# A transformer block on one core: the second MLP starts its halves with products 1 and 2 of both half groups, ends them in another order, keeps pieces of down back, and moves the last layer norm

## The chip, the core and the metric

The kernel runs on one core of a Trainium2 chip. The core has a matrix engine (TensorE, PE in the profile), VectorE (DVE), ScalarE (ACT), GpSimd (POOL) and SyncE (SP), which here only issues DMA transfers. Each engine works through its own queue of instructions in order and waits at semaphores. The metric is the device time of one execution in microseconds. Three runs of the kernel before took 3165.64, 3166.33 and 3169.07 us, so the median is 3166.33 us.

## What is computed

One block over 2048 tokens of width 512, in float32: an MLP, attention with 16 heads of 32, and the same MLP once more, each behind a layer norm and added to its input.

```python
x = x + 0.5 * ffn(layernorm(x))
x = x + attention(layernorm(x))
x = x + 0.5 * ffn(layernorm(x))

def ffn(x):                      # Wg, Wu: 4096 x 512, Wd: 512 x 4096, unpacked from 4-bit codes
    gate, up = x @ Wg.T, x @ Wu.T
    inter = gelu_tanh(gate) * up
    return inter @ Wd.T
```

The first MLP unpacks the weights and keeps them in DRAM; the second MLP, which the change is about, reads them from there.

## The kernel before

**Products.** Every matrix product of the second MLP is done by a scheme that needs 7 products of blocks instead of 8 and pays with additions of blocks. For gate and up it is applied twice: an outer product i in 1..7 is itself made of 7 inner products y in 1..7. The tokens are handled in two halves of 1024. The 4096 columns of the hidden layer are 8 groups g of two half groups h, so a half has 8 x 2 x 7 = 112 outer products. `problems` (L598) lists them, and two at a time form a **pair**: a half has NP = 56 pairs, numbered n = 0..55 in the first half and 56..111 in the second.

**A pair** (`pair`, L705) issues its 7 inner products. Three banks of PSUM, d, f and e, hold the results. Products 1, 6, 7 and 4 go into bank d one after the other, and between them d is read: ScalarE copies it to u1 after product 1 and to u2 after product 6 (L754, L767), VectorE adds d and u5 into the output after product 7 (L770), and only then may product 4 write it, which ScalarE copies out (L776). With pieces of down to interleave the order is 1, 5, 2, 6, pieces "a", 7, 3, pieces "b", 4; without them 1, 5, 6, 2, 7, 3, 4. After the k-th product, the hooks of step k are issued.

**Operands.** The tokens of a half lie transposed in four tiles, called b1, b2, ts and t4 in the code. The outer product i reads x block `(None, 0, 1, 3, 6, 2, 5, 4)[i]` (L699 ff., `factors`): products 1 and 2 read blocks 0 and 1, which are b1 itself; product 3 reads a block of b2; product 5 the difference t1 in b2; 6 and 7 the sums in ts; 4 the one in t4. `outer_sums` (L616) makes ts, t4 and t1 from b1 and b2 with the steps t3, t2, t4, t1. `Tokens.inner(t)` (L684) makes the sums that the inner products 5, 6, 7 and 4 need for the t-th tile; they are called first (b1), second (b2), third (ts) and fourth (t4).

**After a pair.** `recombine(n - 1)` (L777) adds outer products of the pair before into each other (L791), applies gelu on ScalarE (L794) and multiplies gate by up into `inter` blocks (L803). These steps go to steps 1, 4 and 6 of the next pair.

**Down.** When a group is done, `down` (L835) forms four sums of `inter` blocks (L845 to L848, in the tile s, of which there is one) and yields 14 **pieces** of 8 matmuls each (L866). The pieces of group g run inside the seven pairs of group g + 1, by (1, 1, 2, 2, 2, 2, 4) a pair. In the second turn (q = 1) each piece also issues the load of its slot of the next group's down weights (`load_wd`). Results are added to the residual on VectorE (L875) and GpSimd (L881).

**Queue of SP.** At the end of a pair n, `fetch` issues the six transfers of weights for pair n + 4 into a ring of four slots; it waits until pair n has left its slot. All transfers go through SP's one queue, in the order of the program.

**The change of halves.** While the first half ends, the second half's x tiles come back from DRAM (`away`), one of 128 tokens at a time, into buffers `xl`, of which there are three: `load` (L662), `normalize` on ScalarE in place (L941), and `transpose`, four matmuls and a ScalarE copy into b1 or b2 (L949, L950). The eight transpositions stand in pairs 54 to 56. The sums of the new tokens follow in pairs 55 to 57.

**Before and behind.** The second MLP follows attention. In the last of attention's eight passes the first half's layer norm (`Norm`, L116 to L156) stands in the last 16 steps, on VectorE (moments, `xn`), GpSimd (the scales) and TensorE (transposition). Then come 12 pieces of the output projection (L1136), whose results VectorE adds to x (L1140); four of them are copied by ScalarE to tiles `spare` and added on GpSimd (L1143, L1144). After the last pair the kernel runs the last group's 14 pieces and stores the results.

Of the kernel before, what the change touches and what calls it, by code (L numbers as in the profile page):

```python
# [19 lines left out]
P = 128  # L20
# [6 lines left out]
NG = 8  # L27
# [8 lines left out]
def macaron_kernel(ctx: ExitStack, tc: tile.TileContext, x, packed, scales, wqk, bqk, wv, bv, wo, bo, out):  # L36
# [561 lines left out]
    problems = [(g, h, i) for g in range(NG) for h in range(2) for i in (1, 2, 6, 7, 5, 4, 3)]  # L598
# [37 lines left out]
    def second_ffn(finish, ready, slots):  # L636
# [9 lines left out]
        with tc.tile_pool(name="w2", bufs=1) as wp, tc.tile_pool(name="act2", bufs=1) as ap:  # L646
# [13 lines left out]
            def x_away(i):  # L660
                t = ap.tile([P, D], F32, tag="xl", name=f"xl_{next(serial)}", bufs=3)
                nc.sync.dma_start(out=t, in_=away[:, i // 4, (i % 4) * D : (i % 4 + 1) * D])  # L662
                return t
# [3 lines left out]
            class Tokens:  # L667
# [18 lines left out]
                def inner(self, t):  # L686

                    n = 2 if t < 3 else 1
# [94 lines left out]
            def recombine(n):  # L783
# [3 lines left out]
                for g, h, i in pair_of(n):  # L787
# [5 lines left out]
                    def done(row, second, t, g=g, h=h):  # L793
                        gelus.append(lambda: nc.scalar.activation(t[:, 0, :], t[:, 0, :], AF.Gelu_apprx_tanh))  # L794

                        def gate():
                            key = half, g, h, second
                            if row == second:
                                inter[key] = ap.tile(
                                    [P, 2, 512], F32, tag=f"i{h}{second}", name=f"inter_f2_{half}_{g}_{h}_{second}",  # L800
                                    bufs=2 - h,
                                )
                            tt(inter[key][:, row, :], t[:, 0, :], t[:, 1, :], ALU.mult)  # L803

                        gated.append(gate)
# [6 lines left out]
                    elif i == 7:  # L812
                        add(o[7], o[6], nc.gpsimd)
                    elif i == 5:
                        add(o[6], o[5], nc.gpsimd)
                    elif i == 4:
                        add(o[4], o[7])
                        add(o[7], o[5])
                        done(1, 0, o[4])
                        done(1, 1, o[7])  # L820
                    elif i == 3:
                        add(o[3], o[6])
                        done(0, 1, o[3])
# [11 lines left out]
            def down(half, g):  # L835
# [76 lines left out]
                orders = [(1, 2, 6, 5, 7, 3, 4)] * 2 if final else [DOWN, (1, 2, 6, 7, 5, 4, 3)]  # L912
# [51 lines left out]
            first, second, third, fourth = [tokens.inner(t) for t in range(4)]  # L964
            for f in first[2:]:
                f()
            at(0, 0, 0, *third[:2])
            at(0, 0, 1, *third[2:])
            at(0, 0, 3, *second[:2])
            at(0, 0, 5, *second[2:])  # L970
            at(0, 1, 1, *fourth)
# [5 lines left out]
            at(0, 53, 5, call(later.load, 0), call(later.load, 1))  # L977
            at(0, 53, 6, call(later.normalize, 0))
            where = [(0, 54, 1), (0, 54, 4), (0, 55, 0), (0, 55, 3), (1, 0, 0), (1, 0, 2), (1, 0, 4), (1, 0, 6)]
            for i, place in enumerate(where):  # L980
# [19 lines left out]
            for n in range(2 * NP + 1):  # L1000
                mine = {k: hooks.pop((n, k), []) for k in range(7)}
                sums, gelus, gated = recombine(n - 1) if n else ([], [], [])
                mine[1] = sums + mine[1]
                mine[4] = gelus + mine[4]
                mine[6] = gated + mine[6]
                if n == 2 * NP:
                    pieces.pop(0)()
                    for f in mine[1] + mine[4] + mine[6] + down_sums[:2]:
                        f()
                    pieces.pop(0)()  # L1010
# [9 lines left out]
                if pieces:  # L1020
# [3 lines left out]
                    take = 0 if n == NP + 1 else (1, 1, 2, 2, 2, 2, 4)[due]  # L1024
# [4 lines left out]
                if n == NP:  # L1029

                    pieces.pop(0)()
# [5 lines left out]
                if due == 6:  # L1037
                    assert not pieces
                    down_sums, pieces = down(n // NP, n % NP // 7)

    def attention(xT, xT_f, wqk_wv, next_w):
        with tc.tile_pool(name="aw", bufs=1) as aw, tc.tile_pool(name="qk", bufs=1) as qkp, tc.tile_pool(
# [88 lines left out]
            def project_out(u):  # L1131


                def piece(t, copy=None):
# [4 lines left out]
                    if copy is None:  # L1139
                        nc.vector.tensor_tensor(xs[t], po, xs[t], ALU.add)  # L1140
                    else:

                        nc.scalar.copy(copy, po)  # L1143
                        nc.gpsimd.tensor_tensor(xs[t], copy, xs[t], ALU.add)  # L1144

                return [lambda *args, t=t: piece(t, *args) for t in range(NT)]
# [325 lines left out]
            for p in range(NPAIR):  # L1472
# [9 lines left out]
                if p + 1 == NPAIR:  # L1482
# [3 lines left out]
                    for i in range(4):  # L1486
                        extra.setdefault(STARTS[3] + 1 + 2 * i, []).append(o3[4 + i])
                    for tb in range(2):
# [4 lines left out]
                        for i, step in enumerate(norm.steps()):  # L1493
                            after = 2 + i if tb == 0 else (8, 9, 10, 11, 12, 12, 13, 13, 14, 15)[i]
# [35 lines left out]
            t3, t2, t4, t1 = outer_sums(*xT_f, nc.vector)  # L1530
# [7 lines left out]
            for step in [t4] + inner_first(xT_f[0], xT_f[3]):  # L1538
                step()
            spare = [pp.tile([P, 2, 512], F32, tag="pt", name=f"spare_{i}") for i in range(2)]  # L1540
            for i, piece in enumerate(o2[12:] + o3[8:12]):
                if i % 2:
                    piece(spare[i // 4][:, i // 2 % 2, :])
                else:
                    piece()
# [110 lines left out]
```

## Time and profile before

One execution was profiled. It took 3169.56 us, of which the span from the first to the last instruction is 3167.8 us.

| Stretch (us from the span's start) | Length | PE busy | DVE busy | Granted PE clock |
|---|---|---|---|---|
| 2010.00 to 2041.65, end of attention | 31.65 | 29.37 | 23.38 | 0.95 |
| 2052.05 to 2091.06, pairs 0 to 4 | 39.01 | 34.27 | 31.10 | 0.96 |
| 2091.06 to 2551.36, pairs 5 to 53 | 460.30 | 459.92 | | 1.00 |
| 2551.36 to 2611.89, pairs 54 to 57 | 60.53 | 48.71 | 36.32 | 0.89 |
| 2611.89 to 3118.82, pairs 58 to 110 | 506.93 | 506.93 | | 1.00 |
| 3118.82 to 3163.98, pair 111 and the last pieces | 45.16 | 40.30 | 22.48 | 0.92 |

A pair is counted from the start of its product 1. Busy times are those of an engine's instructions; "x4" in a row of the timeline merges four like instructions, and a bracket at its end gives the engine's idle time just before it and what ended that. The granted clock is the share of full speed that TensorE's throttle let through; a busy PE at clock 0.50 does half as much in the same time.

### The profile page before, as it was taken

The page shows a single profiled execution, that of the slowest core. Times are in us where ns is not written, and L with a number is a line of the kernel's source. Part 1 is how long each engine was busy: PE and PEld are TensorE (multiplying, and loading weights), DVE is VectorE, ACT ScalarE, POOL GpSimd, SP SyncE. Part 2 cuts the span into 40 slices and gives each one's busy share as a digit, 9 for nine tenths or more (in the row PEclk, how much of TensorE's full clock was granted, in tenths as well). Part 3 has the DMA queues.
Part 4 walks back from the last instruction along what each step waited for, and adds up shares of the span by engine and source line. Part 5 has one row for each costly group of instructions (what it writes and reads, how often), then busy time and mean ns, then how long its engine had stood idle before and what let it go on. Part 6 is the DMA issues. An engine that isn't in the chain of part 4 may idle for free. (4 is left out here: it accounts for less than half of the span.)

```text
span 3167.8 us, 45167 instructions
## 1 busy us (share of the span) xinstructions
PE 3117.8 (98%) x16592; PEld 2010.6 (63%) x16592; DVE 2050.2 (65%) x3177; ACT 1047.8 (33%) x2074; POOL 1546.1 (49%) x1534
## 2 busy tenths in 40 slices
PE   7999999999999999999999999999999989999998
PEld 3556565656555575444335434478888878888887
DVE  6666666666665755656564566777667667666775
ACT  5111111111111122355453456543333333333332
POOL 3767574857667562455663467522222223223222
PEclk9999999999999999999999999999999999999999
DMA  4223122212122220000000100064444345444441
GB/s 139 79 84 118 71 94 83 97 60 96 67 90 88 84 78 24 5 14 9 12 9 7 30 21 9 13 196 126 132 127 126 118 123 173 119 123 129 130 122 60
DMA packets 261293, 260.21 MB, mean 82 GB/s; under 512 B 21216, under 2 KB 225616, under 8 KB 257104
## 3 DMA queue, kind: packets, MB, share of 16 engines
q1 hardware_dynamic: 261072, 257.33, 25.2%
q8 instruction: 131, 2.15, 0.3%
q14 instruction: 90, 0.74, 0.1%
HBM read 176.28 MB, written 79.92 MB: 81 GB/s over the span
## 5 line engine op out<-in xcount | busy, mean ns | idle before, releaser
L1373 ACT ACTIVATE pt<-ps 128x512 f32<-128x512 f32 (+3 forms) x608 | 288.2, 529 | 180.2 <-PE ps L1348 117.6
L1188 PE MATMUL pm<-kT,qT 32*128 32x512 f32 (+3 forms) x1280 | 333.0, 574 | 0.0
L1200 DVE TENSOR_REDUCE parts<-pm 128x1 f32<-128x512 f32 x384 | 246.4, 685 | 132.1 <-PE pm L1188 131.7
L737 PE MATMUL d_f<-ys_f,ring 128*128 128x256 f32 x1216 | 322.8, 386 | 8.7 <-DVE o_f L770 6.1
L1397 POOL TENSOR_TENSOR sum<-pt,pt 128x512 f32<-128x512 f32 (+1 forms) x225 | 265.5, 1200 | 91.7 <-ACT pt L1373 89.5
L1348 PE MATMUL ps<-qT,kT 32*128 32x512 f32 (+3 forms) x1280 | 277.8, 535 | 0.0
L737 PEld LDWEIGHTS d_f<-ys_f,ring 128*128 128x128 f32 x1216 | 229.0, 192 | 56.3 <-DVE o_f L770 20.6
L438 PEld LDWEIGHTS po<-wd,inter 128*128 128x128 f32 x1024 | 194.4, 190 | 77.5 <-issue 55.0
L791 DVE TENSOR_TENSOR o_f<-o_f,o_f 128x1024 f32<-128x1024 f32 x128 | 203.6, 1601 | 58.0 <-ACT o_f L776 54.2
L438 PE MATMUL po<-wd,inter 128*128 128x256 f32 x1024 | 241.1, 379 | 0.0
L339 PE MATMUL pg<-xT_f,w 128*128 128x512 f32 x512 | 239.4, 595 | 1.1 <-ACT u L378 1.1
L339 PE MATMUL pu<-xT_f,w 128*128 128x512 f32 x512 | 238.0, 592 | 0.0
L452 POOL TENSOR_TENSOR xq<-xq,d 128x512 f32<-128x512 f32 x124 | 162.4, 1321 | 93.8 <-DVE xq L446 58.0
L881 POOL TENSOR_TENSOR xq<-xq,d_f 128x512 f32<-128x512 f32 x48 | 64.7, 1348 | 293.2 <-DVE xq L875 227.7
L791 POOL TENSOR_TENSOR o_f<-o_f,o_f 128x1024 f32<-128x1024 f32 x48 | 128.7, 2682 | 141.1 <-ACT o_f L776 139.8
L881 POOL TENSOR_TENSOR xq_second<-xq_second,d_f 128x512 f32<-128x512 f32 x45 | 61.4, 1364 | 272.3 <-DVE xq_second L875 217.6
L1260 PE MATMUL av<-pt,vals 128*32 128x256 f32 (+1 forms) x2432 | 190.6, 368 | 2.4 <-ACT both L1282 2.3
L393 POOL TENSOR_TENSOR u<-u,u 128x512 f32<-128x512 f32 x64 | 81.7, 1277 | 208.8 <-ACT u L390 208.8
L438 PEld LDWEIGHTS po<-wd,s 128*128 128x128 f32 x768 | 145.5, 190 | 57.9 <-issue 40.2
L438 PE MATMUL po<-wd,s 128*128 128x256 f32 x768 | 181.4, 379 | 0.0
L339 PE MATMUL pg<-xsum,w 128*128 128x512 f32 x384 | 179.2, 596 | 0.0
L339 PE MATMUL pu<-xsum,w 128*128 128x512 f32 x384 | 177.7, 592 | 0.0
(224 smaller groups left out, 6348.6 us busy)
## 6 DMA issues: line engine op xcount, KB each, us to landing
wd_f<-kept SPq DMA_DIRECT2D x112, 256.0 KB
kept<-wd SPq DMA_DIRECT2D x8, 1792.0 KB
xq<-in_x SPq DMA_DIRECT2D x16, 256.0 KB
pk<-in_gate_codes SPq DMA_DIRECT2D x16, 256.0 KB
sc<-in_gate_scales SPq DMA_DIRECT2D x32, 128.0 KB
pk<-in_up_codes SPq DMA_DIRECT2D x16, 256.0 KB
sc<-in_up_scales SPq DMA_DIRECT2D x32, 128.0 KB
pk<-in_down_codes SPq DMA_DIRECT2D x16, 256.0 KB
```

Source lines behind the costliest of these rows:

```text
L339: nc.tensor.matmul(ps, lhsT=a[:, j, :], rhs=b[:, j, :], start=(j == 0), stop=(j == 1))
L438: nc.tensor.matmul(ps[:, j, :], lhsT=a[i][:, k, bass.ts(2 * q + j, P)], rhs=b[i][:, k, :], start=(k == 0), stop=(k == 1),)
L452: adder.tensor_tensor(dst, dst, other, ALU.add)
L737: nc.tensor.matmul(ps[:, k, :], lhsT=fa[k][y], rhs=fb[k][y], start=first and k == 0, stop=True, skip_group_check=True,)
L791: sums.append(lambda: eng.tensor_tensor(dst, dst, other, ALU.add))
L881: adder.tensor_tensor(dst, dst, other, ALU.add)
L1188: nc.tensor.matmul(ps[a][:, :n], lhsT=q[r, bass.ts(4 * g + i, P)], rhs=k[r, kb * 512 : kb * 512 + n], start=True, stop=True,)
L1200: nc.vector.tensor_reduce(most, scores, AX.X, ALU.max)
L1260: nc.tensor.matmul(dst_, lhsT=lhsT, rhs=rhs, start=kw.get("start", False), stop=True, skip_group_check=True)
L1348: nc.tensor.matmul(ps[a][:, off:], lhsT=k[r, bass.ts(c, P)], rhs=q[r, g * 512 + off : (g + 1) * 512], start=False, stop=True,)
L1373: nc.scalar.activation(pt[:, a, plain[a] :], ps[a][:, plain[a] :], AF.Exp, scale=scale)
L1397: eng.tensor_tensor(s[:, a, off_2:], one[:, a, off_2:], other[:, a, off_2:], ALU.add)
```

## The change

- `problems` begins each half with products 1 and 2 of both half groups, so pair n = 1 (and 57) holds products 1 and 2 of h = 1. The last half group of a half takes its products in the order 1, 2, 6, 5, 3, 7, 4, and its additions follow.
- There are two `xl` buffers instead of three. The eight transpositions stand at steps 0, 2, 4, 6 of pairs 54 and 55.
- Sums of tokens are spread to other steps and partly to other engines; `inter` blocks have 2, 2, 2 and 1 buffers instead of 2, 2, 1 and 1.
- Two pieces of down of group 6 are left from pair 55 to pair 56, and three from pair 111 to the end.
- At the end of attention, moments, `xn`, transpositions and four pieces of the projection come at earlier steps, the `spare` path is gone, and t4 of the outer sums moves behind attention.

```diff
-    problems = [(g, h, i) for g in range(NG) for h in range(2) for i in (1, 2, 6, 7, 5, 4, 3)]
+    LAST = NG - 1, 1
+    problems = [(0, 0, 1), (0, 0, 2), (0, 1, 1), (0, 1, 2)] + [
+        (g, h, i)
+        for g in range(NG)
+        for h in range(2)
+        for i in ((1, 2, 6, 5, 3, 7, 4) if (g, h) == LAST else (1, 2, 6, 7, 5, 4, 3)[2 * (g == 0) :])
+    ]
...
-                t = ap.tile([P, D], F32, tag="xl", name=f"xl_{next(serial)}", bufs=3)
+                t = ap.tile([P, D], F32, tag="xl", name=f"xl_{next(serial)}", bufs=2)
...
-                            if row == second:
+                            if key not in inter:
                                 inter[key] = ap.tile(
...
-                                    bufs=2 - h,
+                                    bufs=1 if h == second == 1 else 2,
...
                     elif i == 7:
-                        add(o[7], o[6], nc.gpsimd)
-                    elif i == 5:
+                        add(o[7], o[6], nc.vector if (g, h) == LAST else nc.gpsimd)
+                    elif i == 5 and (g, h) != LAST:
                         add(o[6], o[5], nc.gpsimd)
...
                     elif i == 3:
                         add(o[3], o[6])
+                        if (g, h) == LAST:
+                            add(o[3], o[5])
                         done(0, 1, o[3])
...
-                orders = [(1, 2, 6, 5, 7, 3, 4)] * 2 if final else [DOWN, (1, 2, 6, 7, 5, 4, 3)]
+                late = DOWN if g == NG - 2 else (1, 2, 6, 7, 5, 4, 3)
+                orders = [(1, 2, 6, 5, 7, 3, 4)] * 2 if final else [DOWN, late]
...
-            at(0, 0, 0, *third[:2])
-            at(0, 0, 1, *third[2:])
-            at(0, 0, 3, *second[:2])
-            at(0, 0, 5, *second[2:])
-            at(0, 1, 1, *fourth)
+            at(0, 0, 0, outer_sums(*ready, nc.vector)[2])
+            at(0, 0, 3, *third[:2])
+            at(0, 0, 5, *third[2:])
+            at(0, 1, 2, *second[:2])
+            at(0, 1, 5, *second[2:])
+            at(0, 2, 2, *fourth)
...
-            at(0, 53, 5, call(later.load, 0), call(later.load, 1))
-            at(0, 53, 6, call(later.normalize, 0))
-            where = [(0, 54, 1), (0, 54, 4), (0, 55, 0), (0, 55, 3), (1, 0, 0), (1, 0, 2), (1, 0, 4), (1, 0, 6)]
-            for i, place in enumerate(where):
+            at(0, 52, 5, call(later.load, 0), call(later.load, 1))
+            at(0, 53, 5, call(later.normalize, 0))
+            for i in range(8):
+                place = 0, 54 + i // 4, 2 * (i % 4)
                 at(*place, call(later.transpose, i))
                 if i + 2 < 8:
                     at(*place, call(later.load, i + 2))
                 if i + 1 < 8:
                     at(*place, call(later.normalize, i + 1))
-            t3, t2, t4, t1 = outer_sums(*ready, nc.gpsimd)
-            at(0, 55, 5, *first[:2])
-            at(0, 55, 6, *first[2:])
-            at(1, 0, 6, t3, t2, t4, *third[:3])
-            at(1, 1, 0, third[3])
-            at(1, 1, 1, t1)
-            at(1, 1, 3, *second)
-            at(1, 1, 5, *fourth)
+            t3, t2, t4, _ = outer_sums(*ready, nc.vector)
+            *_, t1 = outer_sums(*ready, nc.gpsimd)
+            at(0, 55, 1, *first[:2])
+            at(0, 55, 3, *first[2:])
+            at(1, 0, 0, t3)
+            at(1, 0, 1, t2)
+            at(1, 0, 4, t4)
+            at(1, 1, 0, t1)
+            at(1, 1, 2, *third[:2])
+            at(1, 1, 4, *third[2:])
+            at(1, 2, 0, *second[:2])
+            at(1, 2, 3, *second[2:])
+            at(1, 2, 0, *tokens.inner(3, nc.gpsimd))
...
-                mine[1] = sums + mine[1]
-                mine[4] = gelus + mine[4]
-                mine[6] = gated + mine[6]
+                for k, steps in zip((2, 5, 6) if n == NP else (1, 4, 6), (sums, gelus, gated)):
+                    mine[k] = steps + mine[k]
                 if n == 2 * NP:
                     pieces.pop(0)()
-                    for f in mine[1] + mine[4] + mine[6] + down_sums[:2]:
+                    for f in sums + gelus:
                         f()
-                    pieces.pop(0)()
+                    for piece in (pieces.pop(0), pieces.pop(1)):
+                        piece()
+                    for f in gated + down_sums[:2]:
+                        f()
+                    for piece in (pieces.pop(0), pieces.pop(0)):
+                        piece()
                     for f in down_sums[2:]:
                         f()
...
-                    take = 0 if n == NP + 1 else (1, 1, 2, 2, 2, 2, 4)[due]
+                    take = {NP - 1: 2, NP: 3, 2 * NP - 1: 1}.get(n, (1, 1, 2, 2, 2, 2, 4)[due])
...
-                if n == NP:
-                    pieces.pop(0)()
...
                     for i in range(4):
-                        extra.setdefault(STARTS[3] + 1 + 2 * i, []).append(o3[4 + i])
+                        extra.setdefault(STARTS[3] + i, []).append(o3[4 + i])
...
-                            after = 2 + i if tb == 0 else (8, 9, 10, 11, 12, 12, 13, 13, 14, 15)[i]
+                            after = ((0, 1, 4, 5, 6, 6, 7, 8, 9, 10), (3, 4, 9, 10, 11, 12, 12, 13, 14, 15))[tb][i]
...
-            for step in [t4] + inner_first(xT_f[0], xT_f[3]):
+            for step in inner_first(xT_f[0], xT_f[3]):
                 step()
-            spare = [pp.tile([P, 2, 512], F32, tag="pt", name=f"spare_{i}") for i in range(2)]
-            for i, piece in enumerate(o2[12:] + o3[8:12]):
-                if i % 2:
-                    piece(spare[i // 4][:, i // 2 % 2, :])
-                else:
-                    piece()
+            for piece in o2[12:] + o3[8:12]:
+                piece()
```

More of the change, by code (lines that the diff above doesn't have):

```diff
@@ L684, in sums, with inner @@
                     return self.operand(x)[:, 0, 256:], t2, t3, t4
-                def inner(self, t):
+                def inner(self, t, eng=nc.vector):
+                    tt = eng.tensor_tensor
                     n = 2 if t < 3 else 1
@@ L961, in call @@
                 return lambda: f(*args)
-            first, second, third, fourth = [tokens.inner(t) for t in range(4)]
+            first, second, third, fourth = [tokens.inner(k) for k in range(4)]
             for f in first[2:]:
                 f()
-            at(0, 0, 0, *third[:2])
-            at(0, 0, 1, *third[2:])
-            at(0, 0, 3, *second[:2])
-            at(0, 0, 5, *second[2:])
-            at(0, 1, 1, *fourth)
+            at(0, 0, 0, outer_sums(*ready, nc.vector)[2])
[4 more added lines that the diff above has]
+            at(0, 2, 2, *fourth)
             for i in range(8):
@@ L1037, in second_ffn @@
                 if due == 6:
-                    assert not pieces
-                    down_sums, pieces = down(n // NP, n % NP // 7)
+                    assert len(pieces) == {NP - 1: 2, 2 * NP - 1: 3}.get(n, 0)
+                    down_sums, new = down(n // NP, n % NP // 7)
+                    pieces += new
     def attention(xT, xT_f, wqk_wv, next_w):
@@ L1131, in project_out, with piece @@
             def project_out(u):
-                def piece(t, copy=None):
+                def piece(t):
                     po = ps_one.tile([P, 512], F32, tag="one", name=f"pp_{u}_{t}")
@@ L1138, in piece @@
                     )
-                    if copy is None:
-                        nc.vector.tensor_tensor(xs[t], po, xs[t], ALU.add)
-                    else:
-                        nc.scalar.copy(copy, po)
-                        nc.gpsimd.tensor_tensor(xs[t], copy, xs[t], ALU.add)
-                return [lambda *args, t=t: piece(t, *args) for t in range(NT)]
+                    nc.vector.tensor_tensor(xs[t], po, xs[t], ALU.add)
+                return [lambda t=t: piece(t) for t in range(NT)]
             def quadrant(p, a):
@@ L1529, in attention @@
             xT_f += [x_transposed("f2_sums", tb) for tb in (2, 3)]
-            t3, t2, t4, t1 = outer_sums(*xT_f, nc.vector)
+            t3, t2, _, _ = outer_sums(*xT_f, nc.vector)
             for step in (t3, t2, outer_sums(*xT_f, nc.gpsimd)[3]):
@@ L1537, in attention @@
                     step()
-            for step in [t4] + inner_first(xT_f[0], xT_f[3]):
+            for step in inner_first(xT_f[0], xT_f[3]):
                 step()
-            spare = [pp.tile([P, 2, 512], F32, tag="pt", name=f"spare_{i}") for i in range(2)]
-            for i, piece in enumerate(o2[12:] + o3[8:12]):
-                if i % 2:
-                    piece(spare[i // 4][:, i // 2 % 2, :])
-                else:
-                    piece()
+            for piece in o2[12:] + o3[8:12]:
+                piece()
             for piece in o3[12:]:
```

## The prediction

> **What bounds the kernel now.** I read the busy shares first, then TensorE's busy time in stretches, then its waits in order of time, then what the waited-for engine was doing, and last the clock.
>
> The page gives the bound, and the stretches (table above) show where it is not met: from pair 5 to 53 and from pair 58 to 110 PE is busy all the time at clock 1.00. There only fewer matmuls would help, and the change keeps their number. All that can move lies in four stretches. The timeline of PE shows their gaps (the bracket: idle before, and its releaser):
>
> ```profile
> PE 3117.8 (98%) x16592; PEld 2010.6 (63%) x16592; DVE 2050.2 (65%) x3177; ACT 1047.8 (33%) x2074; POOL 1546.1 (49%) x1534
> ...
> 2022.07 1.13 PE L155 MATMUL pt_f<-ident,xn_f 128*128 128x128 f32 x4 [2.10 <-DVE xn_f L149]
> ...
> 2056.60 2.07 PE L737 MATMUL d_f<-ys_f,ring 128*128 128x256 f32 x4 [2.66 <-ACT u_f L754]
> ...
> 2586.06 2.07 PE L737 MATMUL d_f<-xT_f_sums,ring 128*128 128x256 f32 x4 [4.09 <-ACT u_f L767]
> 2597.23 1.10 PE L737 MATMUL d_f<-xT_f_sums,ring 128*128 128x256 f32 x4 [2.69 <-issue]
> 2599.77 2.08 PE L737 MATMUL f_f<-xT_f_sums,ring 128*128 128x256 f32 x4 [1.44 <-DVE xT_f_sums L700]
> 2610.92 1.13 PE L737 MATMUL d_f<-ys_f,ring 128*128 128x256 f32 x4 [3.60 <-DVE o_f L770]
> ...
> 3137.35 2.04 PE L866 MATMUL poe_f<-wd_f,inter_f 128*128 128x256 f32 x6 [3.26 <-DVE inter_f L803]
> ```
>
> Two of these are not what they name. In ScalarE's timeline the copy that PE waits for stands behind something else in ScalarE's queue: at the change of halves behind a normalization that waits for an x tile, at the start behind GpSimd's additions from `spare`:
>
> ```profile
> 2055.97 0.58 ACT L754 COPY u_f<-d_f 128x512 f32<-128x512 f32 x1 [6.56 <-POOL xq L1144]
> ...
> 2584.73 0.81 ACT L941 ACTIVATE xl<-xl,nbias,rstd 128x512 f32<-128x512 f32 x1 [4.72 <-DMA xl<-away]
> ```
>
> A matmul after a gap takes 2.07 us for four instead of 1.03. The clock explains it. Windows laid on the throttle's own steps of 3.41 us show (length, PE busy, granted clock):
>
> ```profile
> 2018.72:2022.13 3.41, 1.31 (x25) 1.00 0.00 0
> 2022.13:2025.54 3.41, 3.41 (x16) 0.50 0.00 0
> 2595.57:2598.99 3.42, 1.10 (x4) 1.00 0.26 77
> 2598.99:2605.81 6.82, 6.04 (x14) 0.50 0.16 50
> 2605.81:2609.23 3.42, 1.51 (x7) 1.00 0.05 16
> 2609.23:2612.64 3.41, 1.72 (x8) 1.00 0.00 1
> ```
>
> A window with 1.31 us or less of busy PE is followed by half clock, one with 1.51 is not. So about 2.0 us of idleness within one window cost another 1.7 us.
>
> **The units.** An inner product (4 matmul rows merged) starts 0.86 us after the one before, so a pair is 7 x 0.863 = 6.04; a piece of down 1.73; a transposition 0.47. A pair without pieces takes 6.57 (2096.67 minus 2090.09), since the hand-over of bank d shows.
>
> **End of attention (gain 0.3).** PE lost 2.10 idle and 1.7 of clock. The scales of GpSimd that held `xn` come two steps earlier, so that wait goes. VectorE is late next: before the first `xn` it now also has two more projection adds (0.6 each) and the second block's first moments (1.6), and between first and second `xn` the other moments (1.6). VectorE's queue from 2009.78: 8.4 us of old work, 2.8 us of new, no idle: first `xn` done near 2021.8, second near 2024.0. PE, with one more projection piece (0.94) done by then, arrives at 2020.9: it waits 0.95, transposes, waits 1.7. Sum 2.65 idle against 2.10 plus 1.7, and half a chance of a slow window (0.85). Ends: +3.8 if VectorE keeps up, -2 if every window after is slow.
>
> **Pairs 0 to 4 (gain 3.1).** 39.0 us, of which 5 x 6.57 = 32.85 are work; lost are 2.66, 1.54 of clock (half of the 3.41 at half clock less its idle part), 1.04 and 1.04. GpSimd's `spare` adds go; VectorE gets four adds more (4 x 0.61) and loses t4 (1.69) before them. From 2046.0 its 12 adds end at 2053.3; the last additions in `first` come alone, so at 0.68 each rather than 1.13 and 1.63, and product 6 can start at 2054.05 where PE is ready at 2053.9: 0.15 of wait. The last projection pieces keep GpSimd's divisions (done 2050.47) as cover, 0.8 us before they are needed. t4 (1.2) and half of `third` now stand in pair 0 ahead of the read of bank d: product 4 waits 1.25. `fourth` costs pair 2 some 0.65. The wait of 1.04 behind two L791 adds moves from pair 3 to pair 4. Loss 3.1. The stores to `away` wait for those same adds, so SP reaches pair 2's weights 3 us earlier; pair 2 needs them 4 us earlier, with 4 us of slack before (landed by 2066.4, used at 2070.3). Ends: 0 and +5.
>
> **Pairs 54 to 57 (gain 8.4).** Work: 4 x 6.04, 8 pieces, 8 transpositions, 0.5 for a pair without pieces: 42.2 of 60.5. Lost: 11.8 idle, 6.1 of clock. After, pieces and transpositions number the same, and no pair is bare: 41.7. What goes: the new tokens' sums have one more pair ahead of them, because products 1 and 2 of both half groups need b1 alone, so 2.69, 1.44 and 3.60 go. What comes: with two `xl` buffers the load of tile i + 2 waits for transposition i, and the normalization of tile i + 1 stands in ScalarE's queue at place i, ahead of the u2 copy that product 7 needs. From the start of pair 54:
> - Tile 2 is loaded behind pair 57's six transfers in SP's queue: issue at 3.06, landing 4.36 later (as this load did before: issued 2554.42, landed 2558.78), normalize 0.72, copy 0.58: product 7 at 8.84 where PE is ready at 6.11. **2.73 lost.**
> - Tiles 4 and 5 are issued at the transpositions of 2 and 3 (10.2 and 14.1), land in 3.1, and hold the transpositions of 4 and 5 by **0.55** each.
> - Tile 6 stands behind pair 58's six transfers (3.2 us of SP, from 14.7): issue 17.9, landing 4.55 (as tile 4 did before): product 7 at 23.87 instead of 21.3. **2.57 lost.**
> - Pairs 56 and 57 (17.3 us of PE with 4 pieces) hide the sums, except where GpSimd's t1 and `fourth` run beside VectorE: L845 took 3.37 us beside t1 against 1.22 alone. About **1.0** each in pairs 57 and 58.
> - Clock: a gap of 2.7 us has 2.0 us within one window in 6 of 10 phases: 2 x 0.6 x 1.7 = **2.0**.
>
> Sum 41.7 + 6.4 + 2.0 + 2.0 = 52.1. The Trainium skill, "TensorE: Matmul & The Clock Gate" (HAM oscillation), warns only of idle gaps over about 3.4 us. By it the 2.7 us gaps cost no clock and the gain is 10.4; by the rows above it is 8.4. I take the rows: 2.10 us were enough at 2022. Ends: the loads as slow as the slowest two of before (5.96 instead of 4.36, 3.1, 3.1, 4.55) add 8.8 and leave about -0.4; no wait at all gives +17.8.
>
> **The end (gain 4.7).** 45.2 us from pair 111, of it 6.04 + 18 x 1.73 = 37.1 work. Lost: 3.26 and 1.60 idle, 2.6 of clock. After: the pair keeps one piece (0.15 for its bare half); then one kept piece, a second, piece 1, the third. These 6.9 us cover the last adds, gelus and gates. VectorE runs: the gate that waits for the first kept piece (the single `inter` buffer) and that piece's result, to 3.05 after the pair; three adds to 6.7; gates to 8.1; the first two sums, which also wait for the third kept piece (the single tile s), to 10.55. PE waits 0.3 at piece 2, 1.7 at piece 6, 0.8 at piece 5. Sum 37.3 + 2.8 + 0.3 for GpSimd beside VectorE = 40.4. The kept pieces are 4, 5, 3, so the weights of slots 4, 5, 3 come last: slot 3 is asked for at 6.9, lands 2.7 later, is used at about 16. Ends: +2.5 (a slow window more), +7.5.
>
> Covers: the pair-ahead fetch and the `inter` buffers elsewhere wait for nothing new; down's sums stay in the same steps.
>
> **Sum.** 0.3 + 3.1 + 8.4 + 4.7 = 16.5 us. The profiled execution would go from 3169.56 to 3153.1; against the median of the runs, 3166.33, that is 3149.8, **3150 us**.
>
> **Rivals.**
> - *The x loads hide, no slow window falls.* For it: tile 3 landed in 3.11 and PE has pieces to fill. Against it: ScalarE's order puts the normalization ahead of u2. Then pairs 54 to 57 lose about 1 us: gain 17.8, with 0.3 or more at attention's end, 3.1 and 4.7, 26 in all: 3140.
> - *VectorE becomes the bound where the halves start.* For it: 31.1 of 39.0 us busy in pairs 0 to 4, and additions that triple beside GpSimd. Against it: one more pair to spread them over. If t1 and `fourth` cost PE their whole 5 us and pairs 0 to 2 another 2 to 3: gain 9, 3157.
> - *Slower: two buffers make each reload a round trip that PE waits for.* Four of the six (tiles 2, 4, 5, 6) gate PE, so each further microsecond of landing costs 4. From 8.2 us a landing (4.2 more than assumed) the whole 16.5 is eaten; at 10 us the time is 3166 + 8 = 3174. Against it: the eight loads of this pass landed in 3.1 to 6.0.
> - *The change does nothing there.* The order of the built program shows all moves as described, so this gets no share of its own.
>
> **Chances.** The forecast 0.60, loads hidden 0.20, VectorE 0.14, slower 0.06. The range takes in the second and third and part of the ends above: 3139 to 3159. A change under 0.2% (6.3 us) can't be told from none here: faster 0.88, same 0.06 (several stretches near their low ends at once), slower 0.06.
>
> **What would show it.** Right: no ACT wait for GpSimd L1144 before pair 0; in pairs 54 and 55 two gaps of PE near 2.6 us released by the ScalarE u2 copy, with a normalization behind the DMA ahead of it; pairs 56 and 57 nearly gapless; at the end gaps at pieces 6 and 5 of 1 to 2 us. Wrong: landings of x above 6 us, gaps of PE for VectorE in pairs 0 to 2 above 2 us, or half clock at attention's end for more than one window.

## The result and the profile after

The changed kernel takes 3160.29 us (median of 15 runs, 3158.05 to 3162.29) against 3166.17 us before (15 runs, 3163.63 to 3172.46): ratio 0.9980, 95% interval 0.9972 to 0.9988. It is faster by 5.9 us; 16.5 were predicted, and 3160.3 lies above the range. The profiled execution took 3161.12 us, 8.4 less than that of before.

The page's busy shares, then the windows of the changed kernel (start and end; length; per engine busy time and count; PE clock; share of DMA; GB/s):

```profile
PE 3114.4 (99%) x16592; PEld 2006.8 (64%) x16592; DVE 2055.9 (65%) x3182; ACT 1047.2 (33%) x2070; POOL 1534.8 (49%) x1529
```

```profile
2003.88:2043.72 39.84, 36.13 (x374) 17.56 (x372) 24.86 (x47) 21.27 (x48) 16.45 (x23) 0.91 0.00 1
...
2054.12:2089.13 35.01, 32.83 (x142) 25.36 (x140) 29.78 (x41) 14.75 (x24) 5.76 (x2) 1.00 0.85 271
...
2549.43:2601.34 51.91, 45.04 (x209) 37.97 (x208) 35.10 (x39) 23.16 (x39) 8.70 (x6) 0.97 0.46 137
2601.34:2613.36 12.02, 9.76 (x45) 8.27 (x44) 11.92 (x15) 3.58 (x6) 4.77 (x4) 1.00 0.37 109
...
3110.81:3155.54 44.73, 40.02 (x173) 33.28 (x171) 25.22 (x28) 8.68 (x15) 7.31 (x5) 0.96 0.21 65
```

Laid beside before, stretch by stretch. End of attention is counted from the last projection pieces that both kernels have at the same place (2004.87 before, 2003.88 after) to pair 0, so its length is the first row and the 10.40 us of projection behind it:

| Stretch | Before | After | Gain | Predicted gain |
|---|---|---|---|---|
| end of attention | 47.18 | 50.24 | -3.1 | +0.3 |
| pairs 0 to 4 | 39.01 | 35.01 | +4.0 | +3.1 |
| pairs 54 to 58 (pair 58 took 9.50 before) | 70.03 | 63.93 | +6.1 | +8.4 |
| pair 111 and the last pieces | 45.16 | 44.73 | +0.4 | +4.7 |

These four give 7.4; another 1.0 lies ahead of 2003.88 us, where nothing was changed. The rest of the span is as long as it was. The larger waits of PE in the changed kernel (the bracket: idle before, and its releaser):

```profile
2022.30 0.75 PE L155 MATMUL pt_f<-ident,xn_f 128*128 128x128 f32 x4 [1.30 <-DVE xn_f L149]
...
2025.76 0.26 PE L1357 MATMUL ps<-wo_bo,ones_b 3*128 3x128 bf16 x1 [1.99 <-ACT pt L1391]
...
2557.90 1.13 PE L746 MATMUL d_f<-ys_f,ring 128*128 128x256 f32 x4 [2.18 <-ACT u_f L776]
...
2572.98 1.13 PE L746 MATMUL d_f<-ys_f,ring 128*128 128x256 f32 x4 [1.96 <-ACT u_f L776]
...
2586.03 1.99 PE L877 MATMUL pof_f<-wd_f,s_f 128*128 128x256 f32 x8 [0.69 <-ACT d_f L900]
...
2600.37 1.13 PE L746 MATMUL d_f<-ys_f,ring 128*128 128x256 f32 x4 [1.13 <-DVE o_f L779]
...
2612.39 1.13 PE L746 MATMUL d_f<-ys_f,ring 128*128 128x256 f32 x4 [2.26 <-DVE o_f L779]
...
3126.98 3.68 PE L877 MATMUL pof_f<-wd_f,s_f 128*128 128x256 f32 x8 [2.79 <-ACT d_f L900]
```

The waits of 2.18 and 1.96, in pairs 54 and 55, stand where the prediction put them, and so do the 1.30 and the 1.13. The 1.99, the 0.69, the 2.26 (at this size) and the 2.79 it did not have.

The 1.99 stands at the end of attention, ahead of **scores** (products of queries and keys, L1357 and L1366) of a tile on the diagonal, where a mask is applied: VectorE adds it for one head (L1381), GpSimd selects for the other (L1385). PE waits for ScalarE's exponential (L1391). That one stands in ScalarE's queue behind another, which waits for GpSimd's select:

```profile
2024.86 0.31 ACT L1393 ACTIVATE pt<-pt 128x128 f32<-128x128 f32 x1 [1.40 <-POOL pt L1385]
```

The 2.79 is explained by ScalarE's timeline, too:

```profile
3124.56 0.63 ACT L803 ACTIVATE o_f<-o_f 128x512 f32<-128x512 f32 x1 [4.93 <-DVE o_f L800]
3125.82 0.63 ACT L803 ACTIVATE o_f<-o_f 128x512 f32<-128x512 f32 x1 [0.63 <-DVE o_f L800]
3126.35 0.58 ACT L900 ACTIVATE d_f<-pof_f 128x512 f32<-128x512 f32 x1
```

The third kept piece adds product 3 into bank f, which still holds product 5. ScalarE must read that first (L900), but in its queue the read stands behind two gelus, and these wait for VectorE's last additions. Product 5 had been done at about 3122.5 (its last matmuls started at 3120.57 and took 1.89).

### The profile page after: what moved, and what is told of

Same layout as the page of the kernel before. It is cut to its first block, busy times and chain, and to the rows that moved or that the text cites. A ratio compares the mean times of both kernels' runs of the same rounds, so it can differ in the third digit from the quotient of the medians.

```text
span 3159.3 us, 45153 instructions
## 1 busy us (share of the span) xinstructions
PE 3114.4 (99%) x16592; PEld 2006.8 (64%) x16592; DVE 2055.9 (65%) x3182; ACT 1047.2 (33%) x2070; POOL 1534.8 (49%) x1529
## 4 chain that ended last, share of the span: by engine, by line
PE 93%; DVE 2%; ACT 1%; POOL 1%; issue 1%; DMA 1%; SPq 0%; ACTq 0%; POOLq 0%; DVEq 0%
PE po L438 12%; PE d_f L746 12%; PE pg L339 12%; PE pu L339 12%; PE av L1278 7%; PE pod_f L877 7%; PE pm L1206 6%; PE f_f L746 6%; PE pqk L1122 4%; PE pof_f L877 3%; PE e_f L746 3%; PE ps L1357 2%; PE pv L1139 2%; PE pp L1159 2%; PE poe_f L877 2%; PE ps L1366 1%
## 5 line engine op out<-in xcount | busy, mean ns | idle before, releaser
L1391 ACT ACTIVATE pt<-ps 128x512 f32<-128x512 f32 (+3 forms) x608 | 288.2, 528 | 180.8 <-PE ps L1366 118.5
L1366 PE MATMUL ps<-qT,kT 32*128 32x512 f32 (+3 forms) x1280 | 278.3, 536 | 0.0
L800 POOL TENSOR_TENSOR o_f<-o_f,o_f 128x1024 f32<-128x1024 f32 x44 | 119.2, 2709 | 123.8 <-ACT o_f L785 122.7
```

The costliest lines, as they stand in the source:

```text
L800: sums.append(lambda: eng.tensor_tensor(dst, dst, other, ALU.add))
L1366: nc.tensor.matmul(ps[a][:, off:], lhsT=k[r, bass.ts(c, P)], rhs=q[r, g * 512 + off : (g + 1) * 512], start=False, stop=True,)
L1391: nc.scalar.activation(pt[:, a, plain[a] :], ps[a][:, plain[a] :], AF.Exp, scale=scale)
```

## The experiments

All times are of the same stretches, in the profiled execution of each run, unless a median is named. Each run changes the changed kernel by its diff alone, unless another run is named as its base; run 3 is experiment 3. The longer diffs are shortened.

Medians not named with their run below: 3157.95 us for run 2, 3157.64 (4), 3158.12 (5), 3161.55 (6), 3159.47 (9). The changed kernel's own 15 runs spread over 4.2 us, so differences of 1 or 2 us are read from the stretches and not from these.

**1. Moments 2, 3 and scales of the second block two steps later.** They are one step of the norm, so they move together.

```diff
-  (3, 4, 9, 10, 11, 12, 12, 13, 14, 15)
+  (3, 6, 9, 10, 11, 12, 12, 13, 14, 15)
```

> The changed kernel, but the second block's moments 2, 3 and scales at the end of attention stand at step 6 instead of 4, behind the selects of the first two diagonal tiles in GpSimd's queue. In the changed kernel TensorE takes 45.81 us from the projection piece at 2008.31 to pair 0 (42.74 before the change, from 2009.31), with waits of 0.16, 1.30, 0.17 and 1.99 us and 6.83 us at half clock. Theory (GpSimd: the scales delay the select, the select the exponentials, these the scores of TensorE): the wait of 1.99 falls below 0.7 and the half clock goes; 45.81 becomes 41 to 42.5, the time about 3156. Rival (VectorE: the moments and normalizations came too early, whatever GpSimd does): the wait of 1.30 stays, another of 1 to 2 us comes at the scores, 44.5 to 46, time 3160.

End of attention: 49.03 us instead of 50.24, or 44.6 in the expectation's count. That lies in the rival's range, but not for its reason: the wait of 1.30 that was to stay has gone. The wait at the scores, which the theory was to shorten, stayed at 2.00, and two windows at half clock came all the same (PE timeline of run 1):

```profile
2018.65 1.34 PE L155 MATMUL pt_f<-ident,xn_f 128*128 128x128 f32 x8 [0.17 <-DVE xn_f L149]
...
2022.72 0.26 PE L1357 MATMUL ps<-wo_bo,ones_b 3*128 3x128 bf16 x1 [2.00 <-ACT pt L1391]
```

PE came to the scores earlier, because VectorE no longer had the moments ahead of the second normalized tile, and GpSimd's select came earlier by as much, because the scales were gone from ahead of it. Moments and scales together cost 1.2 us; the share of each was not tried alone. They are not the main thing. Median 3158.76.

**2. Gelus behind the kept pieces.**

```diff
-  for f in sums + gelus: f()
+  for f in sums: f()
   for piece in (pieces.pop(0), pieces.pop(1)): piece()
-  for f in gated + down_sums[:2]: f()
+  for f in gelus + gated + down_sums[:2]: f()
```

> The changed kernel, but after the last pair the two last gelus stand behind the second kept piece and piece 1 in ScalarE's queue instead of ahead of them. In the changed kernel pair 111 and the last pieces take 44.7 us. Theory (the third kept piece, product 3, needs bank f, which ScalarE reads out behind two gelus that wait for VectorE's additions): the wait of 2.79 us ahead of the third kept piece goes, about 1.3 comes at piece 2, the half clock goes; 40 to 41.5 us, the time about 3156.5. Rival (VectorE's chain of additions, gates and sums sets the end, and the next piece waits for it in any case): the 2.79 only moves to pieces 2 and 6, 43 to 44.7 us, time 3159 to 3160.

The wait of 2.79 went, and with it the half clock: 42.10 us, between the two ranges. Waits of 1.08, 1.67 and 1.02 us came at pieces 2, 6 and 5. The timeline of run 2 shows the first of them and, out of the rows of VectorE and GpSimd, what was late for it:

```profile
3126.90 1.56 PE L877 MATMUL poe_f<-wd_f,inter_f 128*128 128x256 f32 x6 [1.08 <-DVE inter_f L812]
...
3122.76 2.22 DVE L800 TENSOR_TENSOR o_f<-o_f 128x1024 f32<-128x1024 f32 x1
...
3122.63 1.27 POOL L892 TENSOR_TENSOR xq_second<-xq_second,d_f 128x512 f32<-128x512 f32 x1 [14.37 <-ACT d_f L900]
```

The addition took 2.22 us where its neighbours took 1.22 and 1.23: GpSimd's ran beside it. That ScalarE's order made the 2.79 is shown; 1.7 us above the predicted 40.4 were still open (runs 11 to 14).

**3. Weights of pairs 57 and 58 asked for behind the x loads.**

```diff
-  mine[6].append(call(fetch, slot(n + 4), pair_of(n + 4)))
+  if n in (NP - 3, NP - 2):
+      at(0, n + 1, 3, call(fetch, slot(n + 4), pair_of(n + 4)))
+  else:
+      mine[6].append(call(fetch, slot(n + 4), pair_of(n + 4)))
```

> The changed kernel, but the weights of pairs 57 and 58 are asked for at step 3 of pairs 54 and 55 instead of at the end of pairs 53 and 54, so the x loads at those places are not behind them in SyncE's queue. Still two x buffers. In the changed kernel pairs 54 to 57 take 51.9 us with waits of 2.18, 0.54, 0.37, 1.96 and 3.4 us at half clock. Theory (the queue of SyncE is the larger part of the round trip): tiles 2 and 6 land 2.4 and 1.6 us sooner, 2.18 and 1.96 fall below 0.5, half clock goes: 46 to 47.5 us; pair 58 takes 12.0 as before or up to 1 more. Rival (two buffers alone: the round trip is waiting for the transposition plus the transfer): both stay above 1.3 and the pairs take 50 to 52. Second rival (VectorE is the bound behind them): the pairs gain, but pairs 57 to 59 lose as much.

Pairs 54 to 57: 45.42 instead of 51.91, no half clock, and pairs 58 and 59 lost nothing. The load of tile 2 left SyncE 1.56 us after the start of pair 54 instead of 3.74, and of ScalarE's waits for x only 0.23 and 0.38 us were left. One wait of PE remained in pairs 54 and 55, for tile 4 (timeline of run 3):

```profile
2561.27 0.75 PE L961 MATMUL pt_later<-ident,xl 128*128 128x128 f32 x4 [1.02 <-ACT xl L953]
```

So SyncE's queue made the two large waits; what is left for the two buffers alone is about 1 us. Three buffers were not tried. Median 3153.28, ratio 0.9958 (0.9943 to 0.9973).

**4. Two sums of pair 58 behind VectorE's read of bank d.**

```diff
-  at(1, 2, 3, *second[2:])
+  at(1, 2, 4, *second[2:])
```

> The changed kernel, but the last two sums of b2's inner operands stand at step 4 of pair 58 instead of step 3, behind VectorE's read of bank d. In the changed kernel pair 58 takes 12.0 us (9.5 are work) with a wait of 2.26 us ahead of its product 4. Theory (VectorE's order at that place): the wait falls to about 0.9, pair 58 to 10.6 us, pair 59 loses nothing. Rival (VectorE is full in pairs 56 to 58, order is not the matter): the wait shows up in pair 59, and both pairs together take as long as now.

Pair 58: 10.69 instead of 12.02, the wait 0.93 instead of 2.26, pair 59 unchanged at 9.50. It was VectorE's order.

**5, 6 and 9. What held the end of attention.** Experiment 5 puts the pieces back to every second step and the moments to 4 and 8; 6 puts the norm's steps back; 9 puts moments 2, 3 and the scales alone back, to step 8.

```diff
-  extra.setdefault(STARTS[3] + i, []).append(o3[4 + i])
+  extra.setdefault(STARTS[3] + 1 + 2 * i, []).append(o3[4 + i])
-  ((0, 1, 4, 5, 6, 6, 7, 8, 9, 10), (3, 4, 9, 10, ...))
+  5: (..., (4, 8, 9, 10, ...))
+  6: ((2, 3, 4, 5, ..., 11), (8, 9, 10, 11, 12, 12, 13, 13, 14, 15))
+  9: (..., (3, 8, 9, 10, ...))
```

> The changed kernel, but the four projection pieces at the end of attention stand at steps 1, 3, 5, 7 as before the change, and the second block's moments at 4 and 8. From the last projection of the group ahead of them to pair 0 TensorE takes 47.18 us before the change, 50.24 after it and 49.03 with the scales alone moved. Theory (the pieces were what TensorE had to do while the first diagonal tiles went through VectorE, GpSimd and ScalarE; at steps 0 to 3 they are used up when that wait comes): the wait of 2.0 us at the scores shrinks to 1 or less, the half clock to one window or none, 45 to 47 us. Rival (the moments and normalizations at earlier steps hold up the diagonal tiles): 49 to 50.5 us.

> The changed kernel, but moments, scales and normalizations at the end of attention stand at the steps of before the change; the four projection pieces stay at steps 0 to 3. Theory (the pieces): the wait at the scores stays near 2 us or more, and the wait for the first normalized tile comes back: 50 to 52 us from the last projection ahead of them to pair 0. Rival (moments and normalizations): 47 to 48 us, as before the change.

> The changed kernel, but the second block's moments 2, 3 and scales at the end of attention stand at step 8, behind all four selects, while the four projection pieces stay at steps 0 to 3. It parts the two halves of the experiment that put pieces and scales back together (47.24 us from the last projection ahead of them to pair 0; 50.25 in the changed kernel, 49.03 with the scales at step 6). Theory (pieces as filler): 48.5 to 50, the wait at the scores stays near 2 us. Rival (the scales in GpSimd's queue are all of it): 47 to 47.7, the wait below 1.

The stretch took 47.24 us in 5, 49.41 in 6 and 49.22 in 9. In 5 a piece stands between the first transpositions, the scores wait 0.72 and one window is at half clock (its PE timeline):

```profile
2019.71 1.02 PE L1159 MATMUL pp<-wo_bo,attnT 128*128 128x512 f32 x2
...
2023.66 0.48 PE L1357 MATMUL ps<-wo_bo,ones_b 3*128 3x256 bf16 x2 [0.72 <-ACT pt L1391]
```

In 9 the scores wait as long as in the changed kernel (its PE timeline), although moments 2, 3 and the scales are out of the way:

```profile
2023.77 0.26 PE L1357 MATMUL ps<-wo_bo,ones_b 3*128 3x128 bf16 x1 [2.01 <-ACT pt L1391]
```

So the pieces had been TensorE's work during the chain of the first diagonal tile (VectorE's mask, ScalarE, GpSimd's select, ScalarE). Moved ahead, they are used up when the wait comes. (Between 9 and 5 the second block's first moments also move, by one step.) The pieces' own share depends on the clock: all ten executions with the pieces at steps 0 to 3 (those of the changed kernel and of runs 1 to 4, 6, 7, 9, 10 and 13) had two windows at half clock here; of the five with the pieces spread (5, 8, 11, 12, 14) four had one, at 47.2 to 47.3 us, and one had two, at 48.55. So the pieces are worth 0.7 us against run 9 where both had two windows, and 2.0 us where they spared one.

In 6 the wait for the first normalized tile was back, and the scores waited only 0.40 (PE timeline of run 6):

```profile
2020.62 0.74 PE L155 MATMUL pt_f<-ident,xn_f 128*128 128x128 f32 x4 [2.40 <-DVE xn_f L149]
```

So neither expectation fits it. But in this stretch run 6 differs from the kernel before in the place of the pieces alone, and it takes 49.41 us where that took 47.18: early pieces cost 2.2 us with the old norm steps, too, of it one more window at half clock. The cost comes at whichever wait is first.

**7. The spare path back.** Four of the last 12 pieces are copied by ScalarE (L1165) and added by GpSimd (L1166) again.

```diff
-  for piece in o2[12:] + o3[8:12]:
-      piece()
+  for i, piece in enumerate(o2[12:] + o3[8:12]):
+      piece(spare[i // 4][:, i // 2 % 2, :]) if i % 2 else piece()
```

> The changed kernel, but four of the last 12 projection pieces are again copied by ScalarE and added by GpSimd, as before the change. Pairs 0 to 4 take 35.0 us in the changed kernel, 39.0 before. Theory (the additions of GpSimd held the first copy of ScalarE and with it TensorE): 37.5 to 39 us, with a wait of 2 to 3 us ahead of the second product of bank d in pair 0 and a window at half clock. Rival (moving the outer sum behind attention and spreading the inner sums brought it): 35 to 36 us.

36.71 us, between the two. The copy again waits for GpSimd, 1.79 us, with no window at half clock (its PE timeline):

```profile
2058.75 1.13 PE L746 MATMUL d_f<-ys_f,ring 128*128 128x256 f32 x4 [1.79 <-ACT u_f L763]
```

So 1.7 of the 4.0 us are the additions of GpSimd. Median 3163.68, ratio 0.9986 (0.9977 to 0.9996). Before, the same wait was 0.9 longer and brought a window at half clock worth 1.5; that the moved sums account for the 0.9 was not tried alone.

**8. All repairs together,** with 2, 3, 4 and 5, and the last additions ahead of the first kept piece.

```diff
...
+  for f in sums: f()
   pieces.pop(0)()
-  for f in sums + gelus: f()
+  for f in late: f()
   for piece in (pieces.pop(0), pieces.pop(1)): piece()
-  for f in gated + down_sums[:2]: f()
+  for f in gelus + gated + down_sums[:2]: f()
```

Here `late` is the gate that waits for the first kept piece.

> The changed kernel with all repairs: projection pieces at steps 1, 3, 5, 7 with the second block's moments at 4 and 8; weights of pairs 57 and 58 asked for behind the x loads; b2's last sums at step 4 of pair 58; at the end the last additions ahead of the first kept piece, a gate that waits for that piece behind it, gelus behind the second kept piece and piece 1. Theory (each is a stretch of its own, so the gains add): end of attention 45 to 47, pairs 0 to 4 35.0, pairs 54 to 57 45.4, pair 58 10.7, pair 111 and the last pieces 38.5 to 40 us; together about 17 us under the changed kernel: 3143, ratio to before 0.9925. Rival (one repair brings forward a wait of another, or the half clock falls elsewhere): 3148 to 3152.

The repairs add: 47.20, 35.00, 46.07 and 10.70 us. Only the end missed, with 42.52: piece 1 waited 1.60 for VectorE's result of the first kept piece, which the additions now stood ahead of. Median 3146.93, ratio 0.9937 (0.9920 to 0.9953): between the 3143 of the theory and the rival's range.

**10. Nothing kept back at the end.**

```diff
-  take = {NP - 1: 2, NP: 3, 2 * NP - 1: 1}.get(n, ...)
+  take = {NP - 1: 2, NP: 3}.get(n, ...)
...
-  for f in sums + gelus: f()
-  for piece in (pieces.pop(0), pieces.pop(1)): piece()
-  for f in gated + down_sums[:2]: f()
-  for piece in (pieces.pop(0), pieces.pop(0)): piece()
+  for f in sums + gelus + gated + down_sums[:2]: f()
+  pieces.pop(0)()
```

> The changed kernel without the pieces kept back at the very end: all four pieces run in pair 111, then piece 1, the last additions, gelus, gates and two sums, and the other pieces, as before the change. Pair 111 and the last pieces take 44.7 us in the changed kernel, 42.1 with the gelus behind the kept pieces. Theory (ScalarE's order ate what keeping back brings): 44 to 45.5 us with one wait of 3 to 4 us at piece 2, about the changed kernel's own. Rival (keeping back brings something as it is): above 46.5. Second rival (the other order of the last products, with one gate less at the end, brings all): 42 to 43.

46.39 us, between the first two: one wait of 3.76 at piece 2 and two windows at half clock, where the changed kernel had one. Keeping back brought 1.7 us in these two profiles. Median 3163.32, ratio 0.9990 (0.9983 to 0.9997), so it brought about 3 us over the runs.

**11 and 12. The end in two more orders,** the rest as in 8. Run 12 moves one line of run 11 (the whole end is shown, without the marks against 8):

```diff
   pieces.pop(1)()               # kept product 5
   for f in sums: f()
   pieces.pop(0)()               # kept product 4
   for f in late: f()
   pieces.pop(0)()               # kept product 3
+  for f in gelus: f()           # 12
   pieces.pop(0)()               # piece 1
-  for f in gelus: f()           # 11
   for f in gated + down_sums[:2]: f()
   pieces.pop(0)()               # piece 2
```

> The run with all repairs once more, with another end: the kept product 5 first, then the last additions, the kept product 4, the gate that waits for it, the kept product 3, piece 1, gelus, gates and sums, piece 2. In the earlier version piece 1 waited 1.60 us for VectorE's result of the first kept piece behind the additions, and the end took 42.5 us. Theory (with product 5 first, bank d is read and bank f copied while other pieces run): 39 to 40.5 us, waits of 0.3 to 0.5 at pieces 2 and 6; the rest as in the earlier version; 3143 to 3146, ratio to before 0.9925 to 0.9935. Rival (GpSimd's addition beside VectorE and the chain of sums set the end): 41.5 to 42.5 us, no gain on the earlier version.

> The second run with all repairs once more, with the two last gelus ahead of piece 1 instead of behind it: there they had been ready at 3108.7 and 3110.9 us but stood in ScalarE's queue behind its read of piece 1 (3113.63). Theory (ScalarE's order is again what piece 2 waits for): the wait of 1.56 us at piece 2 falls to about 0.5, that of 1.48 at piece 6 to about 0.8; pair 111 and the last pieces 40 to 41 us instead of 42.2; 3145.5, ratio to before 0.993. Rival (GpSimd's addition beside VectorE sets it): 41.8 to 42.2 us.

42.18 and 42.77 us: no gain on 8, as the rivals had it, though every step went where it should. In 12 the wait at piece 2 was gone, and 2.20 came at piece 6, with a window at half clock. Medians 3146.97 and 3146.19. The timelines of VectorE and GpSimd in run 12 show what made the sums late:

```profile
3109.21 2.18 DVE L800 TENSOR_TENSOR o_f<-o_f,o_f 128x1024 f32<-128x1024 f32 x1
...
3113.11 2.36 DVE L812 TENSOR_TENSOR inter_f<-o_f 128x512 f32<-128x512 f32 x2
...
3108.47 1.83 POOL L892 TENSOR_TENSOR xq_second<-xq_second,d_f 128x512 f32<-128x512 f32 x1 [12.63 <-ACT d_f L900]
3113.27 1.65 POOL L892 TENSOR_TENSOR xq_second<-xq_second,d_f 128x512 f32<-128x512 f32 x1 [2.96 <-DVE xq_second L886]
```

Without GpSimd beside them the one took 1.22 and the two 1.28 together (VectorE's timeline of run 14):

```profile
3111.86 1.22 DVE L800 TENSOR_TENSOR o_f<-o_f,o_f 128x1024 f32<-128x1024 f32 x1
...
3114.80 1.28 DVE L812 TENSOR_TENSOR inter_f<-o_f 128x512 f32<-128x512 f32 x2
```

**13 and 14. The additions of GpSimd held back** until VectorE's last sum is issued, and then made by VectorE; the stores of their results are held with them. 13 is made on run 2, 14 on run 12.

```diff
-  adder.tensor_tensor(dst, dst, other, ALU.add)
+  if held[0] is None:
+      adder.tensor_tensor(dst, dst, other, ALU.add)
+  else:
+      held[0].append(lambda: tt(dst, dst, other, ALU.add))
...
```

> The run with the gelus behind the second kept piece and piece 1 (end 42.1 us), but the additions that GpSimd made for the kept pieces and piece 2 are held until VectorE's last sum is issued, and made by VectorE. Theory (GpSimd's additions slow VectorE's chain, the chain sets TensorE's waits): no addition of VectorE above 1.3 us at that place, the waits at pieces 2, 6 and 5 (1.08, 1.67, 1.02) fall together by 1.5 to 2.5 us: 39.7 to 40.7. Rival (VectorE's chain is the bound whatever GpSimd does, and three more additions on it cost): 42 to 43 us.

> The third run with all repairs (end 42.8 us, with a wait of 2.20 at piece 6), with the same additions held and made by VectorE. Theory: 39.5 to 40.5 us, the rest as in the earlier runs; 3143 to 3145, ratio to before 0.9925 to 0.993. Rival: 42 us or more, 3146 to 3147.

13: 41.72 us, little under 42.10, and in the median no change (3157.92 against 3157.95). All sums took 1.2 us, but with the old order the additions began late, behind the gate that waits for a kept piece, and a wait of 1.06 for ScalarE's copy came at a later piece. 14: 40.36 us, with waits of 1.12 and 1.04. In the profiles order and GpSimd had to go together; each alone gave little. Of the 2.4 us between 12 and 14, 0.9 are waits and most of the rest is the window at half clock that 14 did not have. In the medians 14 is 1.0 us ahead of 12, less than either spreads. Run 14 beats both kernels: median 3145.16 us (3144.0 to 3146.84), ratio to before 0.9933 (0.9920 to 0.9947).

## Why the prediction was wrong

**Direction right, size wrong.** Faster was forecast and came, but 5.9 us of 16.5. In the profiled executions the four stretches fell 9.1 us short (16.5 less 7.4); the rest is in how far one profile stands for the median (below). Of its own signs of being wrong one came: half clock at attention's end for two windows.

**End of attention: the step that failed.** The prediction followed VectorE's queue and found the right waits: 0.16 and 1.30 for the first and second normalized tile, where 0.95 and 1.7 were given. (One sum was too long: 8.4 and 2.8 us from 2009.78 end at 2021.0, not 2021.8. The first tile was done at 2020.19, which is 2021.2 in the times of the kernel before.) The step that failed is "PE, with one more projection piece (0.94) done by then, arrives at 2020.9". It counted the piece as done early and did not ask what TensorE would do at the next wait, from which the piece was taken. The scores waited 1.99, and two windows ran at half clock where half a chance of one was priced: 3.7 us of waits and 2.8 of clock, where 2.65 and 0.85 were given. Nor did it look at GpSimd's queue, where the second block's scales now stand ahead of the select; with moments 2 and 3 on VectorE they cost 1.2 us (run 1).

**Pairs 0 to 4: right, and somewhat better.** The wait for the spare additions went (run 7). The waits left were 0.96 and 1.04, 2.0 us where 3.1 were given; `fourth` cost nothing.

**Pairs 54 to 58: mechanism right, one size off.** The four waits were 2.18, 0.54, 0.37 and 1.96 for 2.73, 0.55, 0.55 and 2.57, with one window of half clock (1.7) for 2.0. That the two large ones come from SyncE's queue is shown by run 3. The term that was mis-sized is VectorE in pairs 57 and 58, priced at 1.0 each: the wait in pair 57 was 1.13, but pair 58 took 2.5 longer, and 1.3 of that is the place of two sums ahead of the read of bank d (run 4). The 0.69 for ScalarE's copy at a piece of down in pair 56 had no term. The work, taken as 41.7, is 42.6 where no clock is lost (run 3: 45.42 less waits of 2.84); some 0.7 us stay unassigned. (Of the sums, those for tiles 2 and 6 give 8.72 and 23.75, 0.12 less than stated, and no wait at all would have given 18.8, not 17.8.)

**The end: the step that failed.** "These 6.9 us cover the last adds, gelus and gates" took three kept pieces as free to run. Which bank each writes, and who reads that bank in whose queue, was not asked: product 3 needs bank f, and the read stood behind the gelus (run 2: 2.6 us). The term "0.3 for GpSimd beside VectorE" was too small: with GpSimd's additions moved away and the order set, the end takes 40.36 us (run 14). That this is the predicted 40.4 is partly luck: the waits are 2.2 where 2.8 were given, and the rest is 38.2 where 37.6 were.

**The rivals.** VectorE as the bound, at 3157, comes nearest in time, but the losses lay mostly elsewhere. Hidden loads did not occur in the changed kernel. The slower rival needed landings from about 8 us; the six reloads took 2.61 to 4.41.

**Profile and median.** The profiled execution of before lost 6.1 us to half clock at the change of halves, by the prediction's own sum. Executions differ in that: pairs 54 to 57, which runs 1, 2, 4 to 7, 9, 10 and 13 leave as they are in the changed kernel, took 49.8 us there without a window at half clock (run 13) and up to 54.6 with two (run 6). About 3.4 of the 4.8 are the two windows; the rest is longer waits for the same loads (7.9 us of waits in all against 6.4). A gain in clock read from one profile is worth its chance over the phases, not its value there.

## What to carry to other kernels

Before a step is moved ahead, find the wait that it filled: work taken out of a wait's place is missed there, even if the moved step itself costs nothing. For work that is to cover a wait, write down for each piece its bank, who frees that bank, and what stands ahead of that reader in its queue. A load that gates an engine should stand ahead of transfers that have slack in the same queue; here that one move was worth 6.5 us of its stretch.

## What the runs showed of the hardware

**The clock's threshold is sharp.** In the windows of 3.41 us in the pairs and last pieces, in all fourteen experiments and both kernels, every window at full clock with 1.49 us or less of busy PE (26 of them) was followed by half clock, and none with 1.51 or more; the 1.51 is in the prediction's rows. Two such windows of the changed kernel (start and end; length; PE busy and count; PE clock; share of DMA; GB/s):

```profile
2570.67:2574.08 3.41, 1.45 (x8) 1.00 0.44 138
2574.08:2577.49 3.41, 3.41 (x12) 0.50 0.00 0
```

And two of run 10, at the edge, in the same columns:

```profile
2569.08:2572.49 3.41, 1.49 (x9) 1.00 0.42 130
2572.49:2575.90 3.41, 3.41 (x11) 0.50 0.00 0
```

So a gap of 1.9 us can be enough if it lies within one window, and one of 2.26 is free if it straddles two. The wait at 2612.39 shows both. In the changed kernel it straddled two windows (the first two rows); in run 5 the same wait (2.25 us) fell into one, and pair 59 took 11.18 us instead of 9.50 (the last two). So it did in runs 2 and 13:

```profile
2608.21:2611.63 3.42, 1.93 (x9) 1.00 0.00 0
2611.63:2615.04 3.41, 2.65 (x12) 1.00 0.11 31
...
2608.27:2611.68 3.41, 1.43 (x7) 1.00 0.02 5
2611.68:2615.10 3.42, 3.42 (x10) 0.50 0.54 152
```

The prediction weighed this against the Trainium skill, "TensorE: Matmul & The Clock Gate" (HAM oscillation), and its gap of about 3.4 us; here gaps of about 2 us within one window were enough, so the measurements decide. At half clock the five windows with 1.81 to 2.70 us busy were followed by a second one, and those with 3.08 or more were not.

**In attention the limit lies elsewhere.** At the end of attention, where many matmuls use 3 or 32 rows, a window with 2.48 us of busy PE was followed by half clock (run 8's windows, below); among the matmuls of the pairs that never happened above 1.49:

```profile
2019.82:2023.23 3.41, 2.48 (x31) 1.00 0.02 5
2023.23:2026.64 3.41, 3.41 (x28) 0.50 0.00 0
```

Whether it is the rows that count was not tried. Busy time alone doesn't settle it in attention: of the windows near 1209 us with 2.81 or 2.82 us busy, four were followed by half clock (the kernel before and runs 7, 13 and 14), and ten were not.
